# A recurrent cell on one core: column tiles in unbroken turn, and small sums moved from GpSimd to VectorE

## The chip, the cores and the metric

The kernel runs on one core of a Trainium2 chip. The metric is the device time of one execution in microseconds (us); lower is better. The program computes on four engines: TensorE (PE in the profile, its weight loads PEld), VectorE (DVE), ScalarE (ACT) and GpSimd (POOL). SyncE (SP) issues most transfers.

## The reference

A gated recurrence over 512 time steps, with batch 8, input width 512 and state width 512, all in float32, and a residual at the end:

```python
def step(h, x_t):
    fused = sigmoid(concatenate([x_t, h]) @ w_W + w_b)          # 1024 wide
    hidden_state, output_state = split(fused, 2)                # "r" and "z"
    memory_state = x_t @ wx_W + wx_b + hidden_state * (h @ wh_W + wh_b)
    h_new = output_state * h + (1.0 - output_state) * tanh(memory_state)
    return h_new
return x + all h_new            # x is (8, 512, 512), h starts as cond_1024
```

Each step needs the state of the step before. The products with x don't: they can be made ahead of time.

## The kernel before

**Two sorts of products.** The state is the stationary operand of a matmul, 32 columns wide (a group of four steps times a batch of 8), and the weights stream through as the moving operand. An output of 32 rows fills one quarter of the PSUM partitions, so the four quarters (column tiles, `j` = 0 to 3) of the TensorE array work beside one another, each on the weights of another quarter of the units. A float32 matmul appears in the profile as two passes, that is, two MATMUL records with a weight load each.

- *Recurrent products*: per step 12 names in a fixed order, `ORDER = "R0 R1 G0 G1 R2 R3 G2 G3 H0 H1 H2 H3"`. The letter is the PSUM bank (three banks of 128 columns, two sets in turn for groups of four steps, `banks`), the digit the quarter of the state. Quarters 0 and 1 are hTA, 2 and 3 hTB. Each name is four matmuls of 128 columns, one for each column tile, in the order j = 0, 1, 2, 3: 48 matmuls, 96 passes a step.
- *x products* (`products`): for each round `o` of eight steps, seven products from sums of x (`sx`, made by `x_sum`) and sums of weights (`tw`, made by `weight_sum`), which together give what two groups of four steps need with fewer products. Each has two halves of the contraction and four column tiles: 56 matmuls of 192 columns. From step 5 on, every step takes the next seven of them from the generator `later` behind its recurrent products (`take(later, 7)`), so 14 passes. Seven isn't a multiple of four, so the tile with which a step's x products begin moves by three from step to step. The generator is empty after step 500; steps 501 to 511 have recurrent products alone. Steps 0 to 4 take `prefill` matmuls of 384 columns instead.

They accumulate in two more PSUM banks, `xps[0]` and `xps[1]`, in regions called AL, BE (in the first) and GA, DE (in the second).

**One step.** When R is done, VectorE transposes it (tile `tr`, line 371), ScalarE applies the sigmoid, VectorE transposes G and H, and two scans for each half of the state (line 351: tile `m` from `md0` and `md1`, then the new `hTA` or `hTB`) make the products and additions, with tanh on ScalarE between them. The A half comes first, then the B half. The new hTA frees the next step's R0, the new hTB its R2.

**At the end of a step**, in this order in the engines' queues: `load_x` issues a transfer in some steps; `turn_x` transposes one piece of x products for the next group on VectorE; then follow, by the place `u` of the step in its round of eight, ScalarE copies and the GpSimd sums that combine the regions (`odd`, `even`, `both`) and spread them to the banks of the next group (`spread`); in steps 0 to 3 one sum of weights (`weight_sum`, GpSimd, 128x1536 elements); three tiny memsets on VectorE (`idle`); and two GpSimd additions of x to the new state for the output (`ot`, line 495). Engines work through their queues in this order, with a wait where a value is needed.

The lines that matter at u = 2, 3 and 4 (o counts the rounds):

```python
elif u == 2 and nxt:
    last = odd[(o + 1) % 2][:, :HALF]
    nc.scalar.copy(last, reg(GA))
    nc.gpsimd.tensor_tensor(last, last, both, ALU.add)
elif u == 3 and nxt:
    if o:
        nc.scalar.copy(even[:, :HALF], reg(BE))
        nc.gpsimd.tensor_tensor(even[:, :HALF], even[:, :HALF], both, ALU.add)
    spread(2 * o + 2, "R")
elif u == 4 and nxt:
    ...
        x_sum(o + 2, 0)
```

Of the kernel before, what the change touches and what calls it, by code (L numbers as in the profile page):

```python
# [10 lines left out]
ALU = mybir.AluOpType  # L11
PSUM = bass.MemoryType.PSUM

P = 128
NQ = 4
# [17 lines left out]
HALF = 192  # L33

AL, BE = (0, slice(64, 256)), (0, slice(256, 448))
GA, DE = (1, slice(64, 256)), (1, slice(256, 448))
# [5 lines left out]
def tile_cond_rnn_residual(  # L42
# [39 lines left out]
    nc = tc.nc  # L82
# [27 lines left out]
    def x_of(c, k, t, n):  # L110

        e, t = divmod(t, TC // 2)
        if c == 0 and e == 0:
            first = head[:, :NX].rearrange("p (k n) -> p k n", k=NQ)
            return first[:, k, t * B : (t + n) * B]
        return xins[c][:, e, k, t * B : (t + n) * B]
# [17 lines left out]
    def wh(bank, k, j):  # L134
        return whh[:, k, j] if bank == "H" else wgr[:, k, j, {"G": slice(0, 128), "R": slice(128, 256), "Q": slice(0, 256)}[bank]]
# [32 lines left out]
    tw = [const.tile([P, 2, NQ, HALF], F32, name=f"tw{n}") for n in range(4)]  # L168
    sx = [[const.tile([P, 2, GS * B], F32, name=f"sx{n}{q}") for q in range(2)] for n in range(4)]
    step_bias = const.tile([P, HALF], F32, name="stepbias")  # L170
    even = const.tile([P, 256], F32, name="even")
    odd = [const.tile([P, 256], F32, name=f"odd{q}") for q in range(2)]
    both = const.tile([P, HALF], F32, name="both")

    def state(hf, i, slot=2):

        s = i % GS
        return hT[hf][i % NH][:, B * s : B * s + B, :, slot]
# [8 lines left out]
    def mm(out_, lhsT, rhs, start=False):  # L187
        nc.tensor.matmul(  # L188
            out_, lhsT, rhs, start=start, stop=False, skip_group_check=True
        )  # L190
# [13 lines left out]
    for hf in range(2):  # L204
        for slot in (0, 2):
            nc.vector.tensor_copy(
                state(hf, 0, slot), hin[:, 2 * hf : 2 * hf + 2].rearrange("p c b -> p b c")
            )

# [9 lines left out]
    def seed(g):  # L221

        nc.scalar.copy(xps[g % 2], bias)

    def prefill(g):

        c, t0 = divmod(g * GS, TC)
        for k in range(NQ):
            for j in range(NQ):
                mm(  # L230
                    xps[g % 2][32 * j : 32 * j + 32, 64:448],
                    x_of(c, k, t0, GS),
                    wx[:, k, j, :],
                )
            yield

    def late(g):

        if g == 0:
            return xps[0][:, 256:512]  # L240
        return even if g % 2 == 0 else odd[g // 2 % 2]

    def spread(g, names):

        for n in names:
            src = late(g)[:, 128:256] if n == "H" else xps[g % 2][:, XP[n]]
            nc.scalar.copy(banks[g % 2][n], src)
# [7 lines left out]
    def reg(r):  # L255
        return xps[r[0]][:, r[1]]

    def wx_of(kh, ch):
        return wx[:, 2 * kh : 2 * kh + 2, :, HALF * ch : HALF * ch + HALF]
# [2 lines left out]

        return x_of(o // 2, slice(2 * kh, 2 * kh + 2), 8 * (o % 2) + GS * n, GS)

    def weight_sum(n):

        a, b = [
            (wx_of(0, 1), wx_of(0, 0)),
            (wx_of(1, 1), tw[0]),
            (wx_of(1, 1), wx_of(0, 1)),  # L270
            (wx_of(1, 0), tw[1]),
        ][n]
        nc.gpsimd.tensor_tensor(tw[n], a, b, ALU.subtract)

    def x_sum(o, n):

        t_ = [q[o % 2] for q in sx]
        a, b, op = [
            (x_half(o, 1, 0), x_half(o, 1, 1), ALU.add),
            (t_[0], x_half(o, 0, 0), ALU.subtract),  # L280
            (x_half(o, 0, 0), x_half(o, 1, 0), ALU.subtract),
            (x_half(o, 0, 1), t_[1], ALU.subtract),
        ][n]
        nc.gpsimd.tensor_tensor(t_[n], a, b, op)
# [18 lines left out]
    def take(it, n=None):  # L303
        while n is None or n > 0:
            if next(it, it) is it:
                return
            n = None if n is None else n - 1

    def x_side():
        for o in range(2, NG // 2):  # L310
            yield from products(o)
# [3 lines left out]
    warm()  # L315
    later = x_side()
    first = {g: prefill(g) for g in (1, 2, 3)}
    spread(0, "RGH")
    for e in range(NQ):
        turn_x(0, e)  # L320
# [2 lines left out]
    for i in range(T):  # L323
# [8 lines left out]
        for n in (ORDER if i else FIRST).split():  # L332
            if n == "x":
                take(first[1], 1)
                continue
            bank, k = n[0], int(n[1])
            hs = hT[k // 2][i % NH][:, :, k % 2, 2]
            for j in range(NQ):
                to = xps[0][:, :256] if bank == "Q" else ps[bank]
                mm(to[32 * j : 32 * j + 32, :], hs, wh(bank, k, j))  # L340
        if i < 5:
            take(first[(i + 3) // 2], 2)
        else:
            take(later, 7)

        rows = slice(B * s, B * s + B)

# [102 lines left out]
        if u == 0:  # L450
            spread(2 * o + 1, "G")
            if o and nxt:
                nc.scalar.copy(reg(GA), reg(BE))
        elif u == 1:
            spread(2 * o + 1, "H")
        elif u == 2 and o == 0:
            seed(3)
            nc.scalar.copy(even, xps[0][:, 256:512])
        elif u == 2 and nxt:
            last = odd[(o + 1) % 2][:, :HALF]  # L460
            nc.scalar.copy(last, reg(GA))
            nc.gpsimd.tensor_tensor(last, last, both, ALU.add)
        elif u == 3 and nxt:
            if o:
                nc.scalar.copy(even[:, :HALF], reg(BE))
                nc.gpsimd.tensor_tensor(even[:, :HALF], even[:, :HALF], both, ALU.add)
            spread(2 * o + 2, "R")
        elif u == 4 and nxt:
            if o == 0:
                nc.scalar.copy(odd[1], xps[1][:, 256:512])  # L470
            spread(2 * o + 2, "G")
            if two:
                nc.scalar.copy(reg(AL), bias[:, AL[1]])
                x_sum(o + 2, 0)
        elif u == 5 and nxt:
            spread(2 * o + 2, "H")
            if two:
                nc.scalar.copy(reg(DE), step_bias)
                x_sum(o + 2, 1)
        elif u == 6 and two:  # L480
            nc.scalar.copy(reg(BE), reg(AL))
            x_sum(o + 2, 2)
        elif u == 7 and nxt:
            spread(2 * o + 3, "R")
            if two:
                nc.scalar.copy(both, reg(DE))
                x_sum(o + 2, 3)
        if i < 4:
            weight_sum(i)
        if i == 4:  # L490
            nc.gpsimd.tensor_tensor(step_bias, bias[:, BE[1]], bias[:, AL[1]], ALU.subtract)
        for n in range(IDLE):
# [99 lines left out]
```

## Time and profile before

| what | value |
|---|---|
| three runs | 1699.52, 1699.63, 1700.77 us; median 1699.63 |
| profiled execution | 1699.86 us |
| its span, first to last instruction | 1698.1 us |
| TensorE clock granted | 1.00 in the mean |
| PE / PEld busy | 1682.4 / 1623.5 us |
| DVE / ACT / POOL busy | 1127.2 / 974.5 / 384.0 us |
| start, to the first product of step 5 | 40.20 us |
| steps 5 to 500 | 40.20 to 1659.14 us |
| DMA | 31.38 MB, most of it in the first 40 us; 17 GB/s or so afterwards |

The span is what the instructions show; the execution's own time lies 1.76 us above it. Busy time of an engine is the time in which at least one of its instructions ran. In the timeline a row gives start, length, engine, line, operation, output and inputs, shapes and count; in brackets stands the idle time ahead of it and who ended it. Rows of several instructions cover them together. Matmul lines all carry L188, that of the helper `mm`; they are told apart by their tiles (R, G, H from hTA or hTB; xp for the x products).

### The profile page before, as it was taken

To read this page: it belongs to the slowest core of one execution; us is meant where nothing else is said; L and a number is where in the kernel's file an instruction comes from. 1 tells how busy PE (TensorE), PEld (TensorE's weight loads), DVE (VectorE), ACT (ScalarE), POOL (GpSimd) and SP (SyncE) were. 2 spreads that over 40 slices of the span, in tenths; PEclk is the share of its full clock that TensorE was granted. 3 is DMA by queue.
4 is the path that set the end of the run, shared out by engine and by line. 5 is a ranking of instruction groups with operands and counts; after the bars stand their busy time and mean duration, and the time that the engine had idled before them with its cause. 6 is when DMAs were issued, how large, how long until landed. Compare 5 with 4: busy or idle time off the path is not lost.

```text
span 1698.1 us, 129801 instructions
## 1 busy us (share of the span) xinstructions
PE 1682.4 (99%) x56206; PEld 1623.5 (96%) x56206; DVE 1127.2 (66%) x9253; ACT 974.5 (57%) x5946; POOL 384.0 (23%) x1409
## 2 busy tenths in 40 slices
PE   7999999999999999999999999999999999999998
PEld 4999999999999999999999999999999999999997
DVE  6666666666666666666666666666666666666666
ACT  3555555555555555555555555555555555555554
POOL 4222222222222222222222222222222222222221
PEclk9999999999999999999999999999999999999999
DMA  4000000000000000000000000000000000000000
GB/s 176 17 5 18 18 17 17 7 15 17 17 17 17 5 18 17 17 18 5 18 18 17 17 11 11 17 18 17 17 5 18 17 17 17 5 18 11 11 11 10
DMA packets 11524, 31.38 MB, mean 18 GB/s; under 512 B 1220, under 2 KB 1732, under 8 KB 10952
## 3 DMA queue, kind: packets, MB, share of 16 engines
q1 hardware_dynamic: 10800, 22.94, 3.8%
q8 instruction: 439, 7.19, 1.8%
q14 instruction: 133, 1.09, 0.2%
q10 hardware_dynamic: 152, 0.16, 0.0%
HBM read 14.70 MB, written 8.39 MB: 14 GB/s over the span
## 4 chain that ended last, share of the span: by engine, by line
PE 97%; DVE 1%; DMA 1%; ACT 0%; issue 0%
PE R L188 29%; PE H L188 26%; PE G L188 25%; PE xp L188 18%; DMA whh<-in_whh_dram 1%; DVE m L351 0%; DMA rows<-in_bias_dram 0%; DVE md1A L389 0%; DVE hTA L351 0%; ACT hd0A L215 0%; DVE tz L371 0%; ACT hTA L215 0%; DVE rows L120 0%; ACT hTB L215 0%; DVE hTB L351 0%
## 5 line engine op out<-in xcount | busy, mean ns | idle before, releaser
L188 PE MATMUL R<-wgr,hTA 128*32 128x128 f32 x8176 | 409.5, 277 | 6.1 <-DVE hTA L351 6.1
L371 DVE STREAM_TRANSPOSE tr<-R 128x64 f32<-128x64 f32 x1022 | 194.4, 228 | 321.3 <-PE R L188 321.3
L188 PE MATMUL G<-wgr,hTA 128*32 128x128 f32 x8176 | 380.4, 273 | 0.0
L188 PE MATMUL R<-wgr,hTB 128*32 128x128 f32 x8176 | 368.7, 276 | 0.0
L188 PE MATMUL H<-whh,hTA 128*32 128x128 f32 x8192 | 349.6, 273 | 1.0 <-DMA whh<-in_whh_dram 0.8
L188 PE MATMUL H<-whh,hTB 128*32 128x128 f32 x8192 | 349.3, 273 | 0.0
L188 PE MATMUL G<-wgr,hTB 128*32 128x128 f32 x8176 | 348.8, 273 | 0.0
L495 POOL TENSOR_TENSOR ot<-xin,hTB 128x16 f32<-128x16 f32 x503 | 126.7, 252 | 933.6 <-DVE hTB L351 925.5
L188 PEld LDWEIGHTS R<-wgr,hTA 128*32 128x32 f32 x8176 | 275.6, 123 | 30.5 <-DVE hTA L351 22.4
L188 PEld LDWEIGHTS G<-wgr,hTA 128*32 128x32 f32 x8176 | 279.3, 122 | 0.0
L215 ACT ACTIVATE hd0B<-tz 128x16 f32<-128x16 f32 x512 | 116.9, 228 | 280.2 <-DVE tz L371 280.2
L188 PEld LDWEIGHTS H<-whh,hTA 128*32 128x32 f32 x8192 | 271.8, 122 | 1.8 <-DMA whh<-in_whh_dram 1.2
L188 PEld LDWEIGHTS H<-whh,hTB 128*32 128x32 f32 x8192 | 272.0, 122 | 0.0
L188 PEld LDWEIGHTS G<-wgr,hTB 128*32 128x32 f32 x8176 | 271.5, 122 | 0.0
L188 PEld LDWEIGHTS R<-wgr,hTB 128*32 128x32 f32 x8176 | 238.1, 123 | 11.3 <-DVE hTB L351 0.2
L215 ACT ACTIVATE md0A<-tr 128x16 f32<-128x16 f32 x512 | 112.6, 220 | 227.0 <-DVE tr L371 227.0
L351 DVE TENSOR_TENSOR_SCAN hTB<-hd0B,hTB 128x24 f32<-128x24 f32 x1024 | 157.9, 196 | 104.6 <-ACT hTB L215 104.6
L351 DVE TENSOR_TENSOR_SCAN hTA<-hd0A,hTA 128x24 f32<-128x24 f32 x1024 | 157.7, 195 | 103.2 <-ACT hTA L215 103.1
L188 PE MATMUL xp<-tw,sx 128*32 128x192 f32 x2976 | 221.1, 326 | 0.0
L215 ACT ACTIVATE hd0A<-tz 128x16 f32<-128x16 f32 x512 | 115.3, 225 | 111.1 <-DVE tz L371 111.1
L188 PE MATMUL xp<-wx,xin 128*32 128x192 f32 (+1 forms) x2048 | 165.6, 331 | 0.0
L215 ACT ACTIVATE hTB<-hTB 128x16 f32<-128x16 f32 x512 | 119.9, 234 | 79.0 <-DVE hTB L351 67.9
(92 smaller groups left out, 2460.2 us busy)
## 6 DMA issues: line engine op xcount, KB each, us to landing
xin<-in_x_dram SPq DMA_DIRECT2D x31, 256.0 KB, 3.2
out_dram<-ot SPq DMA_DIRECT2D x31, 256.0 KB, 2.4
wx<-in_wx_dram SPq DMA_DIRECT2D x4, 768.0 KB, 7.1
wgr<-in_wgr_dram SPq DMA_DIRECT2D x4, 512.0 KB, 9.7
whh<-in_whh_dram SPq DMA_DIRECT2D x1, 768.0 KB
whh<-in_wh_dram SPq DMA_DIRECT2D x1, 256.0 KB, 11.0
out_dram<-ot SPq DMA_DIRECT2D x1, 192.0 KB, 1.9
head<-in_xh_dram ACTq DMA_DIRECT2D x1, 144.0 KB, 5.1
```

The source lines that it names most:

```text
L188: nc.tensor.matmul(out_, lhsT, rhs, start=start, stop=False, skip_group_check=True)
L215: inst = nc.scalar.activation(out_, in_, func, **kw).ins
L351: nc.vector.tensor_tensor_scan(*[t_[:, :, c_].rearrange("p n c s -> p (n c s)") for t_ in (out_, d0, d1)], 0.0, ALU.mult, ALU.add,)
L371: inst = nc.vector.transpose(t_.rearrange("p c n -> p (c n)"), raw[n][hf]).ins
L495: return engine.tensor_tensor(ot[:, t, 2 * hf : 2 * hf + 2, :].rearrange("p c n -> p n c"), x_of(c, slice(2 * hf, 2 * hf + 2), t, 1).rearr ...
```

## The change

Three things.

1. `turn` counts the x products taken so far. The recurrent products of a step begin with column tile `turn % 4`, not 0, so that the sequence of tiles 0, 1, 2, 3 runs on from a step's recurrent products to its x products and on to the next step's.
2. The sums of weights go from GpSimd to VectorE. Two (numbers 0 and 2) are made whole ahead of step 0, behind the state copies and ahead of `spread` and `turn_x` for the first group. The other two are cut into four chunks of 384 elements each: number 1 behind steps 1 to 4, number 3 behind steps 5 to 8, ahead of the idle memsets.
3. At u = 2 and u = 3 the ScalarE copy of a PSUM region followed by a GpSimd addition becomes one VectorE addition that reads the region and `both`.

```diff
+    turn = [0]
...
-    def weight_sum(n):
+    def weight_sum(n, k=slice(0, 2), j=None):
...
-        nc.gpsimd.tensor_tensor(tw[n], a, b, ALU.subtract)
+        at = (slice(0, P), k, slice(0, NQ) if j is None else slice(2 * j, 2 * j + 2))
+        nc.vector.tensor_tensor(tw[n][at], a[at], b[at], ALU.subtract)
...
     first = {g: prefill(g) for g in (1, 2, 3)}
+    weight_sum(0)
+    weight_sum(2)
     spread(0, "RGH")
...
             for j in range(NQ):
+                j = (j + turn[0]) % NQ
                 to = xps[0][:, :256] if bank == "Q" else ps[bank]
...
             take(later, 7)
+            turn[0] += 7
...
-            nc.scalar.copy(last, reg(GA))
-            nc.gpsimd.tensor_tensor(last, last, both, ALU.add)
+            nc.vector.tensor_tensor(last, reg(GA), both, ALU.add)
...
-                nc.scalar.copy(even[:, :HALF], reg(BE))
-                nc.gpsimd.tensor_tensor(even[:, :HALF], even[:, :HALF], both, ALU.add)
+                nc.vector.tensor_tensor(even[:, :HALF], reg(BE), both, ALU.add)
...
-        if i < 4:
-            weight_sum(i)
+        if 1 <= i < 9:
+            weight_sum(1 if i < 5 else 3, *divmod((i - 1) % 4, 2))
```

## The prediction

> **What bounds the kernel now.** I began with the page: the engine shares, then the chain of work that ended last.
>
> ```profile
> span 1698.1 us, 129801 instructions
> PE 1682.4 (99%) x56206; PEld 1623.5 (96%) x56206; DVE 1127.2 (66%) x9253; ACT 974.5 (57%) x5946; POOL 384.0 (23%) x1409
> PE 97%; DVE 1%; DMA 1%; ACT 0%; issue 0%
> ```
>
> By these lines TensorE is the bound. But "busy" says only that some column tile works. So I read the PE timeline at the joints between steps: a step's last x products (xp), then the next step's first R product. Columns: start, time covered, engine, line, operation, tiles, shape, count.
>
> ```profile
> 689.21 0.33 PE L188 MATMUL xp<-tw,xin 128*32 128x192 f32 x1
> 689.28 0.34 PE L188 MATMUL xp<-wx,sx 128*32 128x192 f32 x2
> 689.30 0.32 PE L188 MATMUL R<-wgr,hTA 128*32 128x128 f32 x1
> 689.37 0.33 PE L188 MATMUL xp<-tw,xin 128*32 128x192 f32 x1
> 689.44 0.61 PE L188 MATMUL R<-wgr,hTA 128*32 128x128 f32 x14
> ...
> 692.73 0.66 PE L188 MATMUL R<-wgr,hTA 128*32 128x128 f32 x16
> 695.91 0.31 PE L188 MATMUL R<-wgr,hTA 128*32 128x128 f32 x1
> ```
>
> Two things. One R pass (689.30) starts ahead of an earlier x pass (689.37): each column tile runs through its own queue, and a break in the order of tiles does not stop the others. And the time from one step's first R to the next differs: 3.43 us, then 3.18. Averaged over the rounds from step 16 on, by step number modulo 8, first R to first R is 3264, 3205, 3257, 3260, 3418, 3184, 3261, 3263 ns, mean 3264. (Steps 5 to 500, 40.20 to 1659.14 us, also give 3264.)
>
> Steps 501 to 511 have no x products:
>
> ```profile
> 1674.93 0.66 PE L188 MATMUL R<-wgr,hTA 128*32 128x128 f32 x16 [0.22 <-DVE hTA L351]
> 1678.09 0.66 PE L188 MATMUL R<-wgr,hTA 128*32 128x128 f32 x16 [0.22 <-DVE hTA L351]
> ```
>
> They take 3156 ns: the recurrence alone (R, transposes, ACT and DVE scans, next hTA). So removing all x work would give only 108 ns a step.
>
> What makes it 3264? Four tiles in parallel start 16 passes of 128 columns every 0.437 us, so a pass holds its tile 109 ns; 16 passes of 384 take 1.29 us (38.91 to 40.20), so one of 192 holds it 161. A product is two passes. Each step gives each tile 12 recurrent products, and with seven x products three tiles get two and one gets one: 24x109+4x161 = 3260 ns on three tiles, 2938 on the other. The short tile's place goes round in four steps, so some tile is long three times running; then the recurrence hands over to another at 3156. No order of issue within a step changes these loads: (3x3260+3156)/4 = 3234 a step. Observed: 3246.5 over remainders 0 to 3, 3281.5 over 4 to 7. Tiles' disorder has at most 12 ns a step to give; the second half of the round loses 35 more on its own.
>
> That loss is on VectorE. POOL and DVE timelines in the step with remainder 4, and the same scan four steps earlier:
>
> ```profile
> 691.82 0.32 POOL L284 TENSOR_TENSOR sx<-xin 128x64 f32<-128x64 f32 x1
> ...
> 691.84 0.44 DVE L351 TENSOR_TENSOR_SCAN m<-md0A,md1A 128x16 f32<-128x16 f32 x2
> 692.47 0.31 DVE L351 TENSOR_TENSOR_SCAN hTA<-hd0A,hTA 128x24 f32<-128x24 f32 x2 [0.19 <-ACT hTA L215]
> ...
> 678.87 0.26 DVE L351 TENSOR_TENSOR_SCAN m<-md0A,md1A 128x16 f32<-128x16 f32 x2
> ```
>
> A scan stands still while GpSimd's sum runs: 0.44 us against 0.26. It does so again, longer, in steps 1 to 3, under the sums of weights (step 4's scan last):
>
> ```profile
> 20.92 3.49 POOL L273 TENSOR_TENSOR tw<-wx,tw 128x1536 f32<-128x1536 f32 x1
> 21.99 2.55 DVE L351 TENSOR_TENSOR_SCAN m<-md0A,md1A 128x16 f32<-128x16 f32 x2
> 25.00 0.66 PE L188 MATMUL R<-wgr,hTA 128*32 128x128 f32 x16 [1.21 <-DVE hTA L351]
> 38.60 0.26 DVE L351 TENSOR_TENSOR_SCAN m<-md0A,md1A 128x16 f32<-128x16 f32 x2
> ```
>
> **The change part by part.** The sum is against the profiled execution, 1699.86 us (span 1698.1 and 1.76 around it), 0.23 above the median 1699.63.
>
> *Weight sums off GpSimd.* First R of steps 1 to 5 stands at 19.69, 25.00, 30.61, 36.16, 40.20: 5.31, 5.61, 5.55 with a sum under them, 4.04 without. All at 4.04: **-4.35 us**.
> Their new cost on VectorE: no row shows such an operation there, so I take the copies of line 203 (128x512 from PSUM, 0.69) and the 128x64 transpose (0.25): 0.98 ns an element. Two whole sums (1536) take 1.7 us each, queued behind the state copies and ahead of the four transposes for step 0. The copies end by 11.4 us at latest (GpSimd's sum stretches a pair to 2.03 now; alone a pair takes 0.25), the sums by 14.8 (TensorE has read all of wx by 12.2), the transposes by 15.3; next on that queue is tr, at 17.40, waiting for TensorE. Cover 2.1 us: nothing; without it 3.4. Eight chunks of 384 take 0.56 each, after steps 1 to 8, in VectorE's idle time before tr: 0.55 (steps 2 to 4), 1.30 (5), 0.55 to 0.65 (later). Queued behind are tr and the chain to hTA. If GpSimd's two ot additions (0.45) hold a chunk up, the four late ones lose up to 0.45 each. From 0 to 1.8: **+0.2**, since these additions start when the chunk does and not before.
>
> *The sums of products.* They free ACT of two copies (0.30 us) and GpSimd of two additions (0.59) in eight steps. ACT's copies stand in idle time: worth 0. GpSimd's addition of remainder 3 starts at 690.86, waiting for ACT's copy, and pushes ot, ot and the sum of x (sx) behind it to 691.41 to 692.14, onto the scan at 691.84. Without it the ot additions follow hTB (690.31), 690.4 to 690.85, and sx ends near 691.2, before any scan. Then remainders 4 to 7 come to what 0 to 3 are: (3281.5-3246.5)x4 = 140 ns, 61 rounds: **-8.5 us**, from 0 (another collision) to -9.5 (the scan's whole 157 ns).
> On VectorE each new sum (192 elements, one operand in PSUM) takes 0.38 by the same rate, 0.30 by ACT's copy of that region. It runs behind the small transpose, before tr, which now follows 0.65 us idle: nothing, since idle exceeds it by 0.27. Without that cover, 0.38 twice in eight steps would be 46 us.
>
> *The turn of tiles.* Between 0 and 12 ns a step: 496x12 = 6 us at most. The one joint without a break today (remainder 0 to 1) enters at 3205, near the recurrence's 3156 and with few late steps, and the three broken ones all stand at 3257 to 3264 although a tile is taken again after one, two or three places: the break itself shows no price. I take **-1.2 us**, a fifth. Below nothing is possible by the same few ns, if the short tile, now first, delays the long ones: +2.
>
> Sum: -4.35+0.2-8.5-1.2 = -13.9, so 1686.0, and against the median **1685.8 us**.
>
> Two rules of the Trainium skill bear on this. "TensorE: Matmul & The Clock Gate", Part 3, states that matmuls keep program order in start and end; the trace differs (689.30 ahead of 689.37). By that rule every break would stall all tiles, and full repair would bring the step to its mean load of 3180 ns or so, some -40 us. "SBUF — State Buffer", section "SBUF: two separate sides", says that a VectorE operation with two SBUF inputs and a GpSimd operation exclude each other for a whole instruction; the stretched scans agree. The new product sums have one PSUM input and would be exempt, the weight chunks not.
>
> **The rivals.**
> *Unbroken order feeds all tiles fully (1654 us).* Mean load (3x3260+2938)/4 = 3180: -84x496 = -41.7, with the start -4.15; the collision is within it: 1653.8. For it: PE's 99% and differing joints. Against: the recurrence's 3156 measured from the latest tile. Chance 0.06.
> *Collision only moves (1694).* GpSimd's sx, earlier, meets another two-input operation of VectorE: -4.15-1.2 = 1694.3. For: ot and sx make 0.77 us, free time from hTB to the next scan is 1.5. Against: that leaves 0.7. Chance 0.12.
> *The new sum of remainder 3 waits for GpSimd (1716).* If it starts after ot, ot, sx (0.77 us), then 0.38+0.77-0.65 = 0.50 late in the one step of four without slack: 61x0.50 = 30 us, so 1716. It is slower than today once the wait passes 0.27+13.9/61 = 0.50 us. For: hTB frees both engines at the same moment. Against: VectorE begins its next operation 0.06 us after the transpose, as ot begins; transposes beside ot run unstretched. Chance 0.07.
>
> **How the numbers follow.** Forecast 0.75, rivals 0.06, 0.12, 0.07. The forecast's own bounds: -4.35-9.5-6 gives 1680, and +1.8+2 with half the collision left gives 1691. The range takes in the moved collision: 1679.5 to 1694.5, leaving out the first and third rivals and the forecast's tail, 2 in 10. This kernel's measurement can tell 0.2%, 3.4 us. Faster: forecast, first rival and most of the second, 0.90; same 0.03; slower 0.07.
>
> **What would show it.** The scans of steps 1 to 3 at 0.26 us, first R of step 5 near 35.9 instead of 40.20. Remainder 4 near 3264, as remainder 0. GpSimd's sx done before the scan. tr idle before it near 0.27 in steps 3 and 4 of a round. Steps with three long tiles still near 3260, the last eleven at 3156. I am wrong if steps fall to 3200, or if remainder 4 stays at 3400 with the scan at 0.26.

## The result, and the profile after

| | before | after |
|---|---|---|
| median of four runs, us | 1699.58 (1699.47 to 1700.77) | 1681.31 (1679.74 to 1682.46) |
| ratio, 95% interval | | 0.989 (0.9873 to 0.9907) |
| profiled execution, us | 1699.86 | 1682.46 |
| its span | 1698.1 | 1679.9 |
| first R of step 5 | 40.20 | 36.64 |
| first R of step 501 | 1659.14 | 1641.21 |
| steps 5 to 500 | 1618.94 | 1604.56 |
| mean step in them, ns | 3264 | 3235 |

The change is faster by 18.3 us, 1.1%. The forecast was 1685.8, with a range from 1679.5 to 1694.5. In the profiled executions the difference of 17.4 us is made of 3.56 at the start, 14.38 in steps 5 to 500 and 0.18 in the tail, less 0.72 by which the time outside the span grew. (Of the 31.38 MB of DMA before, about 7.4 MB, not most, move in the first 40 us, at 185 GB/s against 15 in steps 5 to 500.)

The page of the changed kernel, engine shares and the chain that ended last:

```profile
span 1679.9 us, 129621 instructions
PE 1668.8 (99%) x56206; PEld 1645.4 (98%) x56206; DVE 1144.5 (68%) x9387; ACT 947.4 (56%) x5822; POOL 303.5 (18%) x1281
PE 99%; DVE 1%; DMA 0%; ACT 0%; issue 0%
```

The page looks like the page of before: TensorE at 99%, the rest moved by a few per cent. It can't tell where 17 us went. VectorE gained 134 instructions and 17 us of work, which did not delay it. So I went by stages again.

The start, PE and VectorE timeline of the changed kernel (columns as before):

```profile
24.91 0.62 PE L188 MATMUL R<-wgr,hTA 128*32 128x128 f32 x16
...
28.82 0.62 PE L188 MATMUL R<-wgr,hTA 128*32 128x128 f32 x16
...
32.73 0.62 PE L188 MATMUL R<-wgr,hTA 128*32 128x128 f32 x16
...
36.64 0.62 PE L188 MATMUL R<-wgr,hTA 128*32 128x128 f32 x16
...
25.24 0.52 DVE L275 TENSOR_TENSOR tw<-wx,tw 128x384 f32<-128x384 f32 x1
...
26.47 0.38 DVE L377 STREAM_TRANSPOSE tr<-R 128x64 f32<-128x64 f32 x2 [0.69 <-PE R L188]
...
27.21 0.26 DVE L357 TENSOR_TENSOR_SCAN m<-md0A,md1A 128x16 f32<-128x16 f32 x2
```

Steps 2 to 4 take 3.91 us each, the scan 0.26 (2.55 before). A chunk of a weight sum lies in VectorE's idle time, and 0.69 us of that is left ahead of tr.

VectorE and GpSimd in the step with remainder 4, where the collision was:

```profile
681.19 0.32 DVE L470 TENSOR_TENSOR even<-xp,both 128x192 f32<-128x192 f32 x1
...
681.93 0.38 DVE L377 STREAM_TRANSPOSE tr<-R 128x64 f32<-128x64 f32 x2 [0.40 <-PE R L188]
...
682.67 0.26 DVE L357 TENSOR_TENSOR_SCAN m<-md0A,md1A 128x16 f32<-128x16 f32 x2
...
681.24 0.26 POOL L499 TENSOR_TENSOR ot<-xin,hTB 128x16 f32<-128x16 f32 x1 [2.75 <-DVE hTB L357]
681.45 0.25 POOL L499 TENSOR_TENSOR ot<-xin,hTA 128x16 f32<-128x16 f32 x1
681.66 0.32 POOL L286 TENSOR_TENSOR sx<-xin 128x64 f32<-128x64 f32 x1
```

GpSimd's sx ends at 681.98, and the scan that it used to stretch to 0.44 starts at 682.67 and takes 0.26. VectorE's new sum runs at 681.19 beside ot (0.32 us) and leaves 0.40 us idle ahead of tr.

Mean time from first R to first R, by step number modulo 8, in ns (steps 16 to 495):

| kernel | 0 | 1 | 2 | 3 | 4 | 5 | 6 | 7 |
|---|---|---|---|---|---|---|---|---|
| before | 3264 | 3205 | 3258 | 3261 | 3419 | 3185 | 3261 | 3264 |
| after | 3209 | 3249 | 3252 | 3239 | 3209 | 3236 | 3245 | 3244 |

The spike at remainder 4 is gone, as forecast. Not forecast is that every place is now below the 3257 to 3264 that I had taken for the load of the tiles (3222 to 3261 in a second profile of this kernel, below), while the quick ones of before, 1 and 5, have risen. The tail, steps without x products, is as it was: a median of 3158 before, 3159 after.

### The profile page after: what moved, and what is told of

Same layout as the page of the kernel before. It is cut to its first block, busy times and chain, and to the rows that moved or that the text cites. A ratio compares the mean times of both kernels' runs of the same rounds, so it can differ in the third digit from the quotient of the medians.

```text
span 1679.9 us, 129621 instructions
## 1 busy us (share of the span) xinstructions
PE 1668.8 (99%) x56206; PEld 1645.4 (98%) x56206; DVE 1144.5 (68%) x9387; ACT 947.4 (56%) x5822; POOL 303.5 (18%) x1281
## 4 chain that ended last, share of the span: by engine, by line
PE 99%; DVE 1%; DMA 0%; ACT 0%; issue 0%
PE R L188 27%; PE G L188 26%; PE H L188 26%; PE xp L188 19%; DMA rows<-in_bias_dram 0%; DVE md1A L395 0%; DVE hTA L357 0%; ACT hd0A L216 0%; DVE tz L377 0%; ACT hTA L216 0%; DVE bias L203 0%; DVE rows L120 0%; ACT hTB L216 0%; DVE hTB L357 0%; ACT hd0B L216 0%
## 5 line engine op out<-in xcount | busy, mean ns | idle before, releaser
L188 PE MATMUL R<-wgr,hTA 128*32 128x128 f32 x8176 | 431.5, 275 | 2.4 <-DVE hTA L357 2.2
L188 PE MATMUL G<-wgr,hTA 128*32 128x128 f32 x8176 | 411.9, 273 | 0.0
L188 PE MATMUL R<-wgr,hTB 128*32 128x128 f32 x8176 | 385.9, 275 | 0.0
L188 PE MATMUL H<-whh,hTB 128*32 128x128 f32 x8192 | 366.4, 273 | 0.0
L188 PEld LDWEIGHTS G<-wgr,hTA 128*32 128x32 f32 x8176 | 334.5, 122 | 0.2
L188 PEld LDWEIGHTS R<-wgr,hTA 128*32 128x32 f32 x8176 | 301.2, 123 | 9.0 <-DVE hTA L357 5.5
L188 PEld LDWEIGHTS H<-whh,hTB 128*32 128x32 f32 x8192 | 289.0, 122 | 0.1
L188 PEld LDWEIGHTS H<-whh,hTA 128*32 128x32 f32 x8192 | 289.0, 122 | 0.1
L188 PEld LDWEIGHTS G<-wgr,hTB 128*32 128x32 f32 x8176 | 288.6, 122 | 0.0
L188 PEld LDWEIGHTS R<-wgr,hTB 128*32 128x32 f32 x8176 | 255.2, 123 | 2.2 <-DVE hTB L357 0.5
```

The source lines that it names most:

```text
L188: nc.tensor.matmul(out_, lhsT, rhs, start=start, stop=False, skip_group_check=True)
```

## The experiments

Each kernel was timed in alternation with the kernel before on the same chip, so the ratios compare best; the medians come from four batches, in which the kernel before stood at 1699.6 (the result above), 1702.3 (the first four kernels below), 1701.0 (the next four) and 1702.9 (the last four). The last two columns come from one profiled execution each. "R to hTA" is the median time, at remainders 0 and 4, from the start of R's last pass to tr plus from tr to the end of the first of the scans that write hTA (for the kernel before, remainder 0 alone, since its scan at 4 was stretched).

| kernel | median us | ratio, 95% | step 5 at | steps 5 to 500 | R to hTA, ns |
|---|---|---|---|---|---|
| before | 1699.6 | | 40.20 | 1618.9 | 360+1411 |
| after | 1681.3 | 0.989 (0.9873, 0.9907) | 36.64 | 1604.6 | 310+1411 |
| turn_only | 1696.4 | 0.9962 (0.9951, 0.9974) | 40.99 | 1615.8 | |
| weights_only | 1697.1 | 0.9971 (0.9961, 0.9982) | 35.33 | 1620.0 | |
| sums_only | 1694.4 | 0.9953 (0.9938, 0.9968) | 40.28 | 1613.1 | 360+1409 |
| no_turn | 1688.6 | 0.9921 (0.9906, 0.9936) | 35.36 | 1613.7 | 360+1409 |
| after_again | 1682.5 | 0.9892 (0.9877, 0.9907) | 35.38 | 1605.3 | 310+1411 |
| turn_r | 1688.6 | 0.9927 (0.9910, 0.9943) | 35.37 | 1612.2 | 310+1461 |
| turn_gh | 1684.6 | 0.991 (0.9893, 0.9927) | 35.34 | 1608.4 | 360+1382 |
| late_first | 1688.8 | 0.9927 (0.9912, 0.9942) | 35.71 | 1612.5 | 360+1411 |
| turn_rg | 1686.5 | 0.9901 (0.9887, 0.9916) | 35.57 | 1608.7 | 310+1412 |
| turn_h | 1689.4 | 0.9921 (0.9906, 0.9936) | 35.74 | 1612.2 | 360+1411 |
| xsum_earlier | 1695.1 | 0.9958 (0.9941, 0.9975) | 40.15 | 1613.5 | |
| balanced | 1695.1 | 0.9953 (0.9935, 0.9971) | 35.22 | 1616.3 | |

### The three parts, each alone, and the change without the turn

The three parts were put into the kernel before one by one; no_turn is the changed kernel less the turn.

```diff
  turn_only, on the kernel before
+                j = (j + turn[0]) % NQ
...
+            turn[0] += 7
  weights_only, on the kernel before: the sums of weights, as in the change
-        if i < 4:
-            weight_sum(i)
+        if 1 <= i < 9:
+            weight_sum(1 if i < 5 else 3, *divmod((i - 1) % 4, 2))
...
  sums_only, on the kernel before: the additions at u = 2 and u = 3
+            nc.vector.tensor_tensor(last, reg(GA), both, ALU.add)
...
+                nc.vector.tensor_tensor(even[:, :HALF], reg(BE), both, ALU.add)
  no_turn, on the changed kernel
-                j = (j + turn[0]) % NQ
```

> The turn of tiles alone; sums stay on GpSimd. Steps 5 to 500 took 1618.9 us before and 1604.6 with the whole change. As forecast (the turn is worth 1.2 us): 1617.7, time 1698.4. If instead the shorter gap from the last R pass to tr seen after the change (310 ns in place of 337 to 360) comes from the turn, it saves about 45 ns in four steps, 5.6 us: steps 1613.3, time 1694, remainder 4 still near 3400 with its scan stretched. The theory that breaks stall all tiles wants far more: 1579 for the steps.

> The sums of weights alone go to VectorE. Forecast: first R of step 5 at 36.0 in place of 40.20, steps 5 to 500 unchanged at 1618.9, time 1695.5. The changed kernel has steps 1 to 4 at 3.91, not the 4.04 that I took, so 35.5 is possible where TensorE keeps its full clock in the first wx products. The rival that the chunks hold up tr: first R of step 9 late by up to 1.8.

> The sums of products alone go to VectorE. Forecast: remainder 4 falls from 3418 to 3264 ns and the scan there to 0.26 us, steps 5 to 500 take 1610.4 us, start unchanged, time 1691.1. The rival that the collision only moves: 1618.9 and 1699.6. The rival of a late tr: steps above 1620.

> The whole change without the turn of tiles. If the parts add up: steps 5 to 500 at 1610.4 and first R of step 5 near 35.5 to 36.6, time 1686 to 1687, and the turn is then worth about 5.8 us on top, against the forecast's 1.2. If the turn does nothing: 1604.6 and 1681.

**weights_only** is worth 4.9 us by its ratio (0.0029 of 1699.6; 3.1 to 6.6) and 4.87 by the place of step 5. It leaves the rest alone: remainder 4 stays at 3422.

**sums_only** is worth 8.0 us by its ratio (5.4 to 10.5), and 5.9 by its profile's steps 5 to 500. Remainder 4 falls from 3419 to 3265, but the means of remainders 1 and 5 rise from 3205 and 3185 to 3250 and 3230.

**no_turn** is worth 13.4 us by its ratio, of which 4.8 lie at the start and 5.3 in the steps of its profile. So the turn, on top of it, brings 5 us by the ratios (0.9921 to 0.989) and 8.4 to 9.1 by the steps (1613.7 to 1605.3 and 1604.6). The forecast had 1.2.

**turn_only** gains 6.5 us by its ratio, though the collision is still there in part (remainder 4 at 3332). Its profile's steps give 3.2. The turn is not a small correction.

The steps of one profile hold more than the part that was changed: now and then a step is 50 to several hundred ns longer, and it disturbs its neighbours. The median time of four steps, remainders 0 to 3 and 4 to 7 (62 and 61 such stretches from step 8 to 499, first R to first R), leaves such stretches out. The third column is what the 123 would take at their medians, the last what the profile has beyond that.

| kernel | 0 to 3, ns | 4 to 7, ns | at the medians, us | beyond, us |
|---|---|---|---|---|
| before | 12975 | 13127 | 1605.2 | 0.9 |
| after | 12923 | 12925 | 1589.7 | 2.2 |
| turn_only | 12925 | 13091 | 1599.9 | 3.1 |
| weights_only | 12972 | 13130 | 1605.2 | 2.0 |
| sums_only | 12974 | 12971 | 1595.6 | 4.7 |
| no_turn | 12973 | 12970 | 1595.5 | 5.4 |
| after_again | 12925 | 12925 | 1589.8 | 2.7 |
| turn_r | 12975 | 12973 | 1595.8 | 3.6 |
| turn_gh | 12945 | 12942 | 1592.1 | 3.6 |
| late_first | 12980 | 12980 | 1596.5 | 3.1 |
| turn_rg | 12926 | 12926 | 1589.9 | 6.1 |
| turn_h | 12977 | 12972 | 1595.9 | 3.6 |
| xsum_earlier | 12978 | 12973 | 1596.0 | 4.6 |

By the medians the parts add up: the sums of products bring 9.6 us, all in the half with the collision (13127 to 12971), the turn 5.7 to 5.8 more, 48 ns in every four steps, and the sums of weights nothing in the steps. So the quick steps 1 and 5 gave nothing back in an ordinary round; their means rose through the disturbed ones. Of the 8.4 to 9.1 us between no_turn and the changed kernel 2.7 to 3.2 are such disturbance. Why one profile has more of it than another isn't shown; the kernel before alone stood at medians 3.3 us apart in the four batches.

### The changed kernel once more

> The changed kernel once more, beside the three that follow, since chips differ by some us: steps 5 to 500 at 1604 to 1608 us, 310 ns from the last R pass to tr in every step, 0.989 of the kernel before.

The ratio repeats. What differs between the two profiles is the start: step 5 at 35.38 here, 36.64 above. The stretches of time of the first profile of the changed kernel show why (stretch, length, then busy time and count of PE, PEld, DVE, ACT, POOL, then the granted clock, DMA share and GB/s):

```profile
8.00:9.30 1.30, 0.57 (x2) 0.00 (x0) 0.69 (x3) 0.00 (x0) 0.00 (x0) 1.00 1.04 435
9.30:11.00 1.70, 1.65 (x14) 0.61 (x18) 1.70 (x5) 0.59 (x1) 0.00 (x0) 0.61 0.99 410
11.00:12.20 1.20, 1.20 (x12) 0.42 (x8) 1.20 (x2) 0.00 (x0) 0.00 (x0) 0.50 1.02 416
12.20:14.00 1.80, 1.80 (x17) 0.67 (x10) 0.79 (x1) 0.10 (x1) 0.00 (x0) 0.75 1.03 423
```

By these rows the clock fell short by 0.39 x 1.70 + 0.50 x 1.20 + 0.25 x 1.80 = 1.7 us, that is, TensorE was granted half its clock for 3.4 us; in the second profile the same stretches show 1.00. The first 32 passes with wx took 4.48 us against 2.92 there. That run paid 1.3 us which the same kernel does not pay in the other.

### Is the collision the whole of the second half's loss?

This kernel leaves the copies and GpSimd's additions as they are in the kernel before, and only moves sx of remainder 4 away from the scan.

```diff
         elif u == 2 and nxt:
             nc.scalar.copy(last, reg(GA))
+            if two:
+                x_sum(o + 2, 0)
             nc.gpsimd.tensor_tensor(last, last, both, ALU.add)
...
-                x_sum(o + 2, 0)
+                if o == 0:
+                    x_sum(2, 0)
```

> The kernel before with one thing moved: GpSimd's first sum of x of a round stands two steps earlier, ahead of the addition of remainder 2, where VectorE is idle; ScalarE's copies and GpSimd's additions stay. If only the collision with the scan cost the 140 ns of remainder 4, this alone brings what the product sums on VectorE brought: remainder 4 at 3264, steps 5 to 500 at 1610 to 1613 us, 0.995 of the kernel before. If the copies and additions themselves cost, nothing changes.

Its GpSimd and VectorE timeline, ahead of and in a step of remainder 4:

```profile
688.25 0.60 POOL L468 TENSOR_TENSOR even<-even,both 128x192 f32<-128x192 f32 x1 [2.26 <-ACT even L467]
688.81 0.25 POOL L498 TENSOR_TENSOR ot<-xin,hTB 128x16 f32<-128x16 f32 x1
689.01 0.25 POOL L498 TENSOR_TENSOR ot<-xin,hTA 128x16 f32<-128x16 f32 x1
...
689.24 0.26 DVE L351 TENSOR_TENSOR_SCAN m<-md0A,md1A 128x16 f32<-128x16 f32 x2
```

The slow addition (0.60) and the late ot are still there, but no sx follows them, and the scan takes 0.26. Ratio 0.9958 against 0.9953 of sums_only, steps 1613.5 against 1613.1, remainder 4 at 3267 against 3265. The medians of four steps agree to 5 ns (12978 and 12973 against 12974 and 12971). So the collision of sx with the scan is all that the sums of products had to give; the ScalarE copies and GpSimd additions cost nothing in themselves that these runs can show.

### Where does the turn's gain come from?

In no_turn the time from R's last pass to tr differs by step: 360, 326, 340, 350 ns at remainders 0 to 3. In the changed kernel it is 310 in all. Nothing but the order of the tiles differs.

What the turn does to the order can be worked out from the code: a step that starts with tile t gives its last, seventh x product to t+2, and the next step starts with t+3, the tile that got one product instead of two. The last tile of the next step, t+2, is the one that has been long three times running. So the turn puts the latest tile last in the program, in every step. Without the turn, the latest tile stands in each of the four places in turn.

My first theory: what counts is that R ends with the latest tile. Four kernels turn only some banks, or turn by another amount:

```diff
-                j = (j + turn[0]) % NQ
  turn_r
+                j = (j + turn[0] * (bank == "R")) % NQ
  turn_gh
+                j = (j + turn[0] * (bank != "R")) % NQ
  late_first: the latest tile is first
+                j = (j + turn[0] + 3) % NQ
```

> The changed kernel, but only the R products start at the turned tile; G and H start at tile 0 again, so the joint from H to the x products is broken and a new break stands between R and G. Theory of order: TensorE reports matmuls done in program order, so what counts is that the tile that finishes R last is also the last of R3 in the program; then 310 ns to tr and all of the turn's gain stay: time as the changed kernel within 2 us. Theory of unbroken tiles: the gain goes, 5 to 9 us more than the changed kernel, as without the turn.

> The changed kernel, but the R products start at tile 0; only G and H turn, so that H runs unbroken into the x products. Theory of order: 320 to 360 ns from the last R pass to tr as without the turn, and its whole gain lost: 5 to 9 us over the changed kernel. Theory of unbroken tiles: one of two joints is whole, half the gain stays: 3 to 4 us over it.

> The changed kernel with the turn shifted by three: R now begins with the tile that got the last x product and so ends R last. Theory of order: about 360 ns from the last R pass to tr in all steps, 50 more than with the change; steps 5 to 500 at least as long as without the turn, 7 to 12 us over the changed kernel. Theory of unbroken tiles: breaks as without the turn, 5 to 9 us over it, and the time to tr as it was, 310 to 340.

**The first theory fell.** turn_r has its 310 ns at remainders 0 and 4 (320 to 338 at the others), and keeps nothing: 0.9927 and 1612.2 in the steps, as no_turn (0.9921, 1613.7) within what the runs can tell, and 12975 and 12973 against 12973 and 12970 by the medians of four steps. turn_gh, without a turned R, keeps more (0.991; by the medians 28 of the 48 ns). late_first has 360 in every step and keeps nothing (1612.5).

The timelines say what became of R's 50 ns. First no_turn, step 200, R's and G's last matmuls, then VectorE's transposes of them:

```profile
671.04 0.70 PE L188 MATMUL R<-wgr,hTB 128*32 128x128 f32 x16
671.51 0.66 PE L188 MATMUL G<-wgr,hTB 128*32 128x128 f32 x16
...
671.83 0.38 DVE L374 STREAM_TRANSPOSE tr<-R 128x64 f32<-128x64 f32 x2 [0.62 <-PE R L188]
672.26 0.26 DVE L392 STREAM_TRANSPOSE md1A<-G 128x64 f32<-128x64 f32 x1
```

R ends by the model at 671.04 + 0.70 = 671.74, and tr starts 0.09 us later. G ends at 672.17, and its transpose starts 0.09 later. The same step in turn_r:

```profile
670.35 0.27 PE L188 MATMUL R<-wgr,hTB 128*32 128x128 f32 x1
670.36 0.70 PE L188 MATMUL G<-wgr,hTB 128*32 128x128 f32 x15
...
670.66 0.38 DVE L377 STREAM_TRANSPOSE tr<-R 128x64 f32<-128x64 f32 x2 [0.61 <-PE R L188]
671.15 0.26 DVE L395 STREAM_TRANSPOSE md1A<-G 128x64 f32<-128x64 f32 x1
```

R ends at 670.62 and tr starts 0.04 later: 50 ns won. But G ends at 671.06, its transpose starts 0.09 later, and now stands 0.49 after tr, not 0.43. The wait has only moved from R to G. Hence the second theory: both must end with the latest tile.

```diff
-                j = (j + turn[0]) % NQ
  turn_rg
+                j = (j + turn[0] * (bank in "RG")) % NQ
  turn_h
+                j = (j + turn[0] * (bank == "H")) % NQ
```

> The changed kernel, but H does not turn: x to R and R to G run unbroken, G to H and H to x do not. In the runs with R alone or G and H alone turned, the time from the last R pass to hTA was 1771 (R waits no longer, G does) and 1742 ns, with the whole change 1721. Theory of order, mended: R and G must both end with the late tile last in the program; then 1721 here, steps 5 to 500 at 1605 to 1607 us, 0.989 of the kernel before. Theory of unbroken tiles: two joints broken, 1610 or more, 0.992.

> The changed kernel, but only H turns, so that H runs unbroken into the x products and R and G start at tile 0. Theory of order: 1771 ns from the last R pass to hTA where a round hands over, steps 5 to 500 at 1612 to 1614 us as without the turn, 0.992 of the kernel before. Theory of unbroken tiles: that joint is the one that counts, 1608 or less, 0.990.

The same step in turn_rg:

```profile
668.49 0.69 PE L188 MATMUL R<-wgr,hTB 128*32 128x128 f32 x15
668.90 0.71 PE L188 MATMUL G<-wgr,hTB 128*32 128x128 f32 x16
...
669.23 0.38 DVE L377 STREAM_TRANSPOSE tr<-R 128x64 f32<-128x64 f32 x2 [0.62 <-PE R L188]
669.66 0.25 DVE L395 STREAM_TRANSPOSE md1A<-G 128x64 f32<-128x64 f32 x1
```

0.05 us each, and the transpose of G stands 0.43 after tr. (turn_gh lies between: R's 360 stay, G comes 29 ns sooner, 1742 in sum against the 1769 to 1771 of no_turn, turn_r, late_first and turn_h, and the 1721 of turn_rg.) turn_rg comes to 0.9901 and 1608.7, turn_h to 0.9921 and 1612.2. An unbroken joint from H to the x products, which turn_h has, gains nothing by itself; R and G turned together have 5.0 of the 8.4 to 9.1 us in the steps, most of it by the ratio (0.9901 against 0.989, overlapping intervals), and all of it by the medians of four steps: 12926 against the changed kernel's 12923 to 12925.

50 ns at the hand-over, once in four steps, make 496/4 x 0.050 = 6.2 us, near the 5.7 to 5.8 of the medians. The two measures move together: from the last R pass to hTA 1769 to 1771, 1742 and 1721 to 1722 ns go with four steps of 12970 to 12980, 12942 to 12945 and 12923 to 12926. The 3.4 us by which turn_rg's steps exceed after_again's lie in disturbed stretches (6.1 against 2.7 us); turning H adds nothing to an ordinary round. Open is why the reader is released 50 ns earlier. That TensorE reports its matmuls in program order, so that an early tile late in the program holds a bank's last word back, would fit 310 and 360, but no run shows it directly.

### Loads of the tiles made equal

If three long tiles and a short one set the step, dealing the x products to pairs of tiles, one in seven cut into halves of 96 columns, should bring each tile to its share.

```diff
+    SHARES = (
+        (("01", 0, whole), ("23", 0, whole), ("01", 1, whole), ("23", 1, left)),
+        (("23", 1, right), ("01", 2, whole), ("23", 2, whole), ("01", 3, whole)),
...
-            take(later, 7)
-            turn[0] += 7
+            take(later, 1)
+            turn[0] = (2, 2, 0, 0)[(i - 5) % 4]
```

> The changed kernel with the x products of four steps dealt out by tile: in two steps tiles 0 and 1 get two products and tiles 2 and 3 one and a half, in the next two the reverse; for that one product in seven is made in two halves of 96 columns (32 matmuls in four steps, not 28), and a step's R begins with the tiles that were freed first. Theory of loads: a tile is long (3271 ns) for two steps running, not three, and in between a round can gain nothing but the hand-over of 3126: (3271+3126)/2 = 3198 a step in place of 3236, so steps 5 to 500 take 1586 us, 0.978 of the kernel before. If loads of tiles are not the limit, more matmuls and more breaks make it no faster: 1605 or more, 0.989 to 0.993.

It is slower than the changed kernel: 0.9953, steps 1616.3, mean step 3259. In rounds without a pause its steps alternate as the loads say, about 3160 and 3260 from tr to tr (mean 3210 from the medians, less than the changed kernel's 12924/4 = 3231). But between the starts of its passes there are 41 pauses of over 180 ns, 12.3 us in sum, where the changed kernel has 3. One of them is in this line of its PE timeline (14 passes in 0.98 us, where 13 take 0.60 elsewhere):

```profile
700.59 0.98 PE L188 MATMUL R<-wgr,hTB 128*32 128x128 f32 x14
701.30 0.70 PE L188 MATMUL G<-wgr,hTB 128*32 128x128 f32 x16
```

Most of the distances between pauses are multiples of 128 passes within 2 (383, 640, 511, 639, 383 and so on). 128 passes with their weight loads are 256 instructions, and the transfer queues of its page, here ahead of the changed kernel's, show instructions brought in packets of 7.32 MB / 447 = 16 KB:

```profile
q8 instruction: 447, 7.32, 1.9%
q8 instruction: 439, 7.19, 1.7%
```

For 1984 instructions more (131605 against 129621) it brings 8 packets more, 248 instructions to a packet. The other profiles have such pauses too, 1 to 11 of them in steps 5 to 500, and in all that have more than one the distances are multiples of 127.8 passes within 1.3. So the pauses look like TensorE waiting for its program. That is argued from the distances and was not tried by itself. The pauses account for 12 of the 24 us by which the steps exceed 496 x 3.210 = 1592; the rest is open. No version that I ran was faster than the changed kernel.

## Why the prediction was right, and where not

The time lies inside the range, 4.5 us below the forecast (18.3 gained where 13.9 was forecast). The mechanisms of the two larger terms were right. All three brought more than forecast: the weight sums by the place of step 5, the other two by the medians of four steps. That the total is no further below the forecast is luck: in the profiled execution the clock and the disturbed stretches took some 2.6 us back.

- **Weight sums, forecast -4.35 and +0.2.** Measured -4.87 by weights_only's step 5, -3.56 in the profiled run, 1.3 of whose start went to the clock. The 4.04 us that I took for a free step was not free: in weights_only steps 1 to 4 take 4.02 and three times 3.91, 15.75 in all for 20.51, and step 1 begins 0.11 sooner. Costs on VectorE were close: chunks 0.515 us for 0.56, whole sums 1.754 for 1.7. The +0.2 did not show.
- **Sums of products, forecast -8.5.** In sums_only remainder 4 fell by 154 ns and four steps with it by 156 (13127 to 12971), nearly the scan's whole 157: 9.6 us at the medians, just past the bound of 9.5. The forecast's 140 came from means, which hold disturbed stretches. By sums_only's steps, with 4.7 us of these where the kernel before had 0.9, the term is 5.9, by its ratio 8.0. The new sum takes 0.316 us (0.30 to 0.38 forecast), and leaves 0.36 to 0.40 of idle time ahead of tr, more than the 0.27 forecast. That it runs unstretched beside ot agrees with the Trainium skill, "SBUF — State Buffer", section "SBUF: two separate sides", by which a VectorE instruction with at most one SBUF input does not contend with GpSimd. The second rival, of a moved collision, and the third, of a sum waiting for GpSimd, did not come.
- **The turn of tiles, forecast -1.2, bound 6.** This is the term that was mis-sized: 5.7 to 5.8 us by the medians of four steps, 5 by the ratios, 8.4 to 9.1 in the steps with their disturbance. The bound held by the medians, 12 ns a step. The step that failed is "the break itself shows no price. I take -1.2 us, a fifth". The break indeed has no price (turn_h, turn_rg), and the loads do not change, as the prediction says; but the order of the tiles changes the hand-over, which the prediction took at the tail's 3156 without asking what the order does to it. From R's last pass to tr it is 310 ns against 360, with 340 in the tail. I read the joints for a price of the break and, finding none, stopped; I did not look at the reader of R, for which the same timeline had shown 360, 338, 346 and 352 ns. So the floor "(3x3260+3156)/4 = 3234 a step" came out near (12924/4 = 3231), but the changed kernel reaches it for a reason that the prediction does not have.
- **The forecast's bounds.** The 1691 "with half the collision left" is a wrong sum: 1685.8 with 1.6 and 3.2 more is 1690.6 with the whole collision gone; with half of it left it is 1694.8, just outside the range. The measured time lies far from that end.
- **Full feeding, 1654.** Not so: 3235 a step, not 3180. The Trainium skill, "TensorE: Matmul & The Clock Gate", Part 3, has matmuls start in program order. In the changed kernel as in the one before, an R pass still starts ahead of x passes that stand before it, and the measurement decides:

```profile
689.87 0.31 PE L188 MATMUL R<-wgr,hTA 128*32 128x128 f32 x1
689.89 0.36 PE L188 MATMUL xp<-tw,sx 128*32 128x192 f32 x3
```

- **What would show it.** Scans at 0.26 and remainder 4 equal to remainder 0 came true, and step 5 "near 35.9" lies between the two profiles' 35.38 and 36.64. The last eleven steps stayed (3159). "Steps with three long tiles still near 3260" did not: the medians from tr to tr are 3270 at six remainders of no_turn, and 3206 to 3253 at all eight in the changed kernel, where the hand-over is no longer at one remainder.

## What to carry to other kernels

When several queues run beside one another and one reader waits for all, issue the queue that is furthest behind last, and do so for each result on the reader's path: fixing one of two only moves the wait to the other. A single profile's total over hundreds of steps also holds disturbance that differs from profile to profile; the median of a whole round (here four steps) tells what a change is worth in an ordinary round. And before a gain is booked against a step called free, look for a second row that is really free.

## What the runs showed of the hardware

- The time from a bank's last pass to its reader depended on the order in which the column tiles stood in the program, 310 to 360 ns, with the number and shape of the passes unchanged. Where R and G both had the shorter time, four steps took 12923 to 12926 ns; where they did not, 12942 to 12980 (kernels without the collision).
- The granted clock of TensorE fell to half for 3.4 us near the start in two of fourteen profiles (from 9.7 us in the profiled run of the changed kernel, 1.3 us of its time; from 8.9 us in turn_only), and stayed at full there in the second profile of the changed kernel.
- Pauses of 180 to 980 ns between the starts of passes came at multiples of 127.8 passes within 1.3, 1 to 11 of them in steps 5 to 500; with 32 matmuls for 28 in four steps there were 41, of 189 to 549 ns.
